# Two depthwise convolutions and the weight set-up of a two-layer state-space kernel: diagonal products for one convolution, set-up moved into the planned schedule

## The chip, the cores and the metric

The kernel runs on one core of a Trainium2 chip. Its time is the device time of one execution in microseconds; several executions are made and the median is given. Besides, one execution is recorded by the hardware profiler. The core has five engines with instruction queues of their own: TensorE (PE in the profile, its weight loads as PEld), VectorE (DVE), ScalarE (ACT), GpSimd (POOL) and SyncE (SP), which here only starts DMAs. A name with a q, such as SPq or ACTq, is an instruction that an engine's queue issues, a DMA above all.

## The reference, cut to what matters

The input is x of 4 images with 256 channels and 64 x 64 points, so 4 sequences of 4096 tokens. Layer 0 is a selective state-space block with a causal convolution of 4 taps in front of its recurrence. Layer 1 is a state-space block with 8 heads and scalar decays, again with such a convolution, and after it a feed-forward layer with 8 experts, each token going to one of them. The two convolutions are what the change touches:

```
# layer 0: xm has 512 channels
xp = jnp.pad(xm, ((0, 0), (K - 1, 0), (0, 0)))
xc = sum((xp[:, k:k + L, :] * conv_w[:, k] for k in range(K))) + conv_b
xm = jax.nn.silu(xc)
...
# layer 1: xBC has 512 channels of x and 128 of B and C
xpad = jnp.pad(xBC, ((0, 0), (D_CONV - 1, 0), (0, 0)))
conv = sum((xpad[:, k:k + L, :] * conv_w[:, k] for k in range(D_CONV))) + conv_b
xBC = jax.nn.silu(conv)
```

Everything is float32. A convolution here is depthwise: each channel has its own 4 weights.

## The kernel before, in words

**Phases.** Three phases follow one another: `mixers` (both state-space layers and the routing of the tokens), `experts` (71 blocks of 256 tokens through the feed-forward layer), and `turn` (the result is turned back to channels first and written out). The change lies in `mixers` alone.

**Chunks.** `mixers` works on 64 chunks of 256 tokens, 16 per sequence. For a chunk, `front0` (L712) makes the projections of layer 0 and its convolution, `mid0` (L764) the step sizes and inputs of the recurrence, `scan` (L824) the recurrence itself as 16 scans of 128 x 1024 on VectorE, `tail0` (L902) the output projection. `front1` (L924) makes the normalization, projections and convolution of layer 1, `ssd` (L1037) its state step in two halves of 128 tokens, and `back1` (L1127) its output, the choice of expert and the scatter of the rows into the routing buffer. Layer 1 works two chunks behind layer 0 (`lag = 2`, L1232).

**The order of the work.** `mixers` does not issue its instructions where they are written. `r` is a `Plan` (L136): each call of `r.mm`, `r.act`, `r.dve`, `r.gps` or `r.dma` notes an operation with a slot, and `k_.at(n)` sets the slot to 16 times the chunk's number plus n. `Plan.order` (L273) then goes through a simulated time: on each engine it starts the operation with the lowest slot that is ready and for whose tiles a buffer is free. The cost of an operation is charged by formulas in `mm`, `act`, `dve` and `gps` (L207 to L248). For `mm` with over 64 output rows this is `max(0.224, n / 592)` us, with up to 32 rows `max(0.15, n / 1500)`; for `dve` it is 0.06 us plus n / 960, and 0.14 instead of 0.06 where n is at most 4. The queues that come out are fixed: each engine takes its instructions in this order. All instructions of the plan are issued at one line, L371, so the profile tells them apart by tile names only.

**Buffers.** A tile has a ring with a name and a number of buffers. `raw`, the input of a convolution with 3 columns of the chunk before in front of it, is one buffer for both layers; `raw4` has three, `z` and `xn1` one each. In PSUM, layer 0 takes its banks from ring a (two), layer 1 from ring b (one), the state step from ring c (two).

**The convolution before.** Both layers do it alike. `to_taps` (L677) stores `raw` to DRAM as `raw_d`; `tapped` (L683) loads it back four times for each of 4 blocks of 128 channels, shifted by one column each time, so that the 128 partitions of `raw4` hold 4 taps of 32 channels; `convolve` (L693) makes 4 products with 128 rows of input and 32 columns of weights, each for 32 channels. The weights, `taps_m` for layer 0 and `taps_x` for layer 1, are made at the start by GpSimd from `sum4` (four 32 x 32 identities on top of one another) and the tap weights (L517). The much smaller convolution of B and C in layer 1 uses diagonal matrices, `diag_bc` (L510, L1019): 4 products of 128 x 128 that add up in PSUM, one for each tap, reading `rbc` at four shifts.

**The set-up before.** L442 to L596 stand ahead of the plan, so their instructions are the first in every queue. The weights of layer 0 are loaded from SP (L442 to L456), those of layer 1 from ScalarE's queue (L460 to L474). ScalarE has the Exp of `neg_a0` (L457) in front of these loads and the Exp of `neg_a1` (L475) behind them. Then come the products that fold the input projection and the means into the weights (L527 to L570), and those of layer 1 and of the gate (L573 to L592).

Of the kernel before, what the change touches and what calls it, by code (L numbers as in the profile page):

```python
# [20 lines left out]
P = 128  # L21
T = 256
# [82 lines left out]
class Root:  # L105


    def __init__(self, ring, depth, make, psum):
        self.ring, self.depth, self.make, self.psum = ring, depth, make, psum
        self.tile = self.first = None  # L110
        self.seen = []
        self.left = 0
        self.until = 0.0
        self.begun = ring is None

    def place(self):
        if self.tile is None:
# [18 lines left out]
class Plan:  # L136
# [30 lines left out]
    def note(self, engine, weight, f, args, kw, outs, ins, join=None, lag=0.0, port=False, ride=False):  # L167
        op = self.ops[-1] if join is not None and self.open == (join, self.now) else None
        if op is None:
            op = Op(len(self.ops), engine, self.now, self.step)  # L170
            self.ops.append(op)
        self.open = (join, self.now) if join is not None else None
        op.calls.append((f, args, kw))
        op.weight += weight
        op.lag = max(op.lag, lag)
        op.port, op.ride = op.port or port, op.ride or ride
        for parts, writes in ((ins, False), (outs, True)):
            for p in parts:
# [12 lines left out]
                root.seen.append((op, writes, p.box))  # L191
        return op


# [35 lines left out]
    def dve(self, name, *args, **kw):  # L230
        out, *rest = (*args, *kw.values())
        tensors = [a for a in rest if isinstance(a, Part) or hasattr(a, "ap")]
        n = max(self.width(a) for a in (out, *tensors))
        port = len([a for a in tensors if self.on_sbuf(a) and self.width(a) > 1]) > 1
        if name == "tensor_tensor_scan":
            n, port = 2 * n, False
        op = self.note("DVE", (0.06 if n > 4 else 0.14) + n / 960, getattr(self.nc.vector, name), args, kw, (out,), rest, port=port)
        op.scan = name == "tensor_tensor_scan"
        if op.scan:
            self.scans.append(op)  # L240
# [141 lines left out]
def tile_conv_attn_hybrid(ctx: ExitStack, tc: tile.TileContext, a: dict, out: bass.AP, cap: int, st: int):  # L382
# [12 lines left out]
    def nm(s):  # L395
        return f"{s}_{next(names)}"
# [27 lines left out]
    def mixers(es):  # L424
# [16 lines left out]

        w_in = load("w_in")  # L442
        w_gate = load("w_gate")
        b_gate = load("b_gate")
        ln_g = load("ln_g")
        ln_b = load("ln_b")
        m_in = load("m_in_w")
        m_cw = load("m_conv_w")
        m_cb = load("m_conv_b")
        m_xp = load("m_xproj_w")  # L450
        m_dtw = load("m_dt_w")
# [2 lines left out]
        m_d = load("m_D")  # L454
        m_out = load("m_out_w")
        w_out = load("w_out")  # L456
        act(neg_a0, neg_a0, AF.Exp)  # L457
        ts(neg_a0, neg_a0, -1.0, None, ALU.mult)

        s_in = wp.tile([P, KC, 2 * DI + 2 * N2 + NH + NE], F32, name="w_W_in", tag="w_W_in")  # L460
        nc.scalar.dma_start(s_in[:, :, :-NE], a["W_in"])
        s_cw = load("conv_w", nc.scalar)
        s_cb = load("conv_b", nc.scalar)
        s_cwbc = load("conv_w_bc", nc.scalar)
        s_cbbc = load("conv_b_bc", nc.scalar)
        s_dtb = load("dt_bias", nc.scalar)
        neg_a1 = load("A_log", nc.scalar)
        s_d = load("Dp", nc.scalar)
        s_gn = load("gnorm_w", nc.scalar)
        s_nw = load("norm_w", nc.scalar)  # L470
        s_out = wp.tile([P, KD, C + NE], F32, name="w_W_out", tag="w_W_out")
        nc.scalar.dma_start(s_out[:, :, :C], a["W_out"])
        g_w = load("gate_w", nc.scalar)
        g_b = load("gate_b", nc.scalar)  # L474
        act(neg_a1, neg_a1, AF.Exp)  # L475
        ts(neg_a1, neg_a1, -1.0, None, ALU.mult)

        for k in range(KC):
            ts(s_in[:, k, :-NE], s_in[:, k, :-NE], s_nw[:, k : k + 1], None, ALU.mult)
        for k in range(KD):  # L480
            ts(s_out[:, k, :C], s_out[:, k, :C], s_gn[:, k : k + 1], None, ALU.mult)
# [27 lines left out]
        diag_d1 = diagonal(s_d, "diag_d1")  # L509
        diag_bc = diagonal(s_cwbc, "diag_bc")  # L510
# [6 lines left out]
        def taps(scales, name):  # L517

            t = wp.tile([P, NG, R], F32, name=name, tag=name)
            for g in range(NG):  # L520
                nc.gpsimd.tensor_scalar(t[:, g], sum4, scales[:, g : g + 1], None, ALU.mult)
            return t
# [50 lines left out]
        g_cen = g_w  # L573
        pt_s = bank_a()
        for k in range(KC):
            mm(pt_s[:, :NE], mean_c, g_w[:, k], start=k == 0, stop=k == KC - 1)
        for k in range(KC):
            tt(g_cen[:, k], g_w[:, k], pt_s[:, :NE], ALU.subtract)

        nc.scalar.copy(s_in[:, :, -NE:], g_cen)
        for k in range(KD):
            pt_s = bank_a()
            for m in range(KC):
                nc.tensor.transpose(pt_s[:, m * P : (m + 1) * P], s_out[:, k, m * P : (m + 1) * P], ident)
            turned = wk.tile([P, KC, P], F32, name=nm("turned"), tag="sq", bufs=1)
            nc.scalar.copy(turned, pt_s[:, :C].rearrange("p (m l) -> p m l", m=KC))
            pt_s = bank_a()
            for m in range(KC):  # L590
                mm(pt_s[:, :NE], turned[:, m], g_cen[:, m], start=m == 0, stop=m == KC - 1)
            nc.scalar.copy(s_out[:, k, C:], pt_s[:, :NE])  # L592
# [38 lines left out]

        def scratch(shape, tag):
            return r.tile(lambda: dram2.tile(shape, F32, name=nm(tag), tag=tag), shape, tag, 3)

        routed, rows_at, ws_at = r.fixed(buf_d), r.fixed(row_at), r.fixed(w_at)

# [75 lines left out]
        def front0(k_):  # L712
# [28 lines left out]
            for half in range(2):  # L741
# [182 lines left out]
        def front1(k_):  # L924
# [510 lines left out]
def layouts(i):  # L1435
# [13 lines left out]

    def by_tap(w):  # L1450

        return np.asarray(w).reshape(NG, R, TAPS).transpose(2, 1, 0).reshape(P, NG)

    def spread(v):
# [24 lines left out]
        "conv_w": by_tap(at["conv_w"][:DI]),  # L1479
# [46 lines left out]
```

## Time and profile before

| | us |
|---|---|
| median of 3 executions | 6781.04 (6777.89 to 6788.52) |
| the profiled execution, its time | 6786.87 |
| its span, first to last instruction | 6785.2 |
| mean granted TensorE clock in it | 0.934 of full speed |

One instruction of TensorE on float32 appears as two passes in the profile, so the counts there are twice those of the code. A mean duration of a TensorE pass [...]overlaps with the pass after it; busy time is the union. A wait is put down to the engine and tile whose work came last before the waiting instruction started. The largest group of VectorE is the scans, 1024 of 2284 ns; the largest of GpSimd the product of the states with C (`p<-h,bc`), 1024 of 2357 ns; the largest of ScalarE the decays (`da<-dt,w_m_Alog`), 4096 of 502 ns. On the DMA side, the loads `raw<-raw_d` of both convolutions are 2048 transfers of 128 KB with a median of 3.8 us from issue to landing, and the stores `raw_d<-raw` are 128 of 518 KB with 4.2 us.

### The profile page before, as it was taken

The numbers are of one execution on the slowest core, as the hardware profiler recorded it, in microseconds if no ns is written. First come the engines' busy times: TensorE is split into PE (matmuls) and PEld (weight loads), VectorE is DVE, ScalarE is ACT, GpSimd is POOL, SyncE is SP. The second block draws the span as 40 slices with busy tenths as digits, with TensorE's granted clock in tenths as the row PEclk, the third lists the DMA queues.
The fourth block names the chain that finished last, engine by engine and source line by source line (L and its number), as shares of the span: only waits on it lengthen the run. The fifth ranks groups of instructions, "written<-read, shape, count | busy, mean of one in ns | idle before, by whom it ended". The sixth has DMA issues, their size and how long they took to land. (4 is left out here: it accounts for less than half of the span.)

```text
span 6785.2 us, 114276 instructions
## 1 busy us (share of the span) xinstructions
PE 5984.4 (88%) x37672; PEld 4045.8 (60%) x37672; DVE 5545.7 (82%) x7646; ACT 4859.2 (72%) x12007; POOL 3494.2 (51%) x2632
## 2 busy tenths in 40 slices
PE   5788888888888888888888888888888877999996
PEld 3455555555555555555555555555555546888885
DVE  3889999999999999999999999999999973344333
ACT  4778888888888888888888888888888852333332
POOL 3555555555555555555555555555555552333331
PEclk7889999999999999999999999999999988999998
DMA  6976777777777777777777777777777734555556
GB/s 177 254 184 179 183 181 181 181 184 184 181 181 177 180 181 183 184 182 182 183 182 183 183 183 181 184 183 183 183 183 181 178 102 152 193 193 191 187 194 243
DMA packets 1125138, 1245.58 MB, mean 184 GB/s; under 512 B 111888, under 2 KB 1093652, under 8 KB 1115330
## 3 DMA queue, kind: packets, MB, share of 16 engines
q1 hardware_dynamic: 1083458, 1008.76, 59.1%
q0 software_dynamic: 30000, 210.98, 8.8%
q10 hardware_dynamic: 11088, 18.53, 0.7%
q8 instruction: 300, 4.92, 0.3%
q14 instruction: 292, 2.39, 0.1%
HBM read 919.92 MB, written 311.63 MB: 182 GB/s over the span
## 5 line engine op out<-in xcount | busy, mean ns | idle before, releaser
L371 POOL TENSOR_TENSOR p<-h,bc 128x1024 f32<-128x1024 f32 x1024 | 2413.3, 2357 | 1995.3 <-DVE ub L371 578.3
L371 DVE TENSOR_TENSOR_SCAN h<-da,ub 128x1024 f32<-128x1024 f32 x1024 | 2338.9, 2284 | 80.4 <-ACT da L371 4.8
L371 ACT ACTIVATE da<-dt,w_m_Alog 128x255 f32<-128x255 f32 x4096 | 1830.7, 502 | 0.5 <-issue 0.5
L371 DVE TENSOR_TENSOR ub<-u,bc 128x1024 f32<-128x1024 f32 x1024 | 1269.1, 1239 | 20.2 <-DMA u<-u_d 11.3
L371 PE MATMUL py<-p,sum 128*32 128x256 f32 x8192 | 689.6, 411 | 334.1 <-POOL p L371 326.3
L371 PE MATMUL b<-t,w_W_in 128*128 128x256 f32 x2304 | 581.5, 393 | 65.1 <-ACT raw L371 26.1
L371 PEld LDWEIGHTS py<-p,sum 128*32 128x32 f32 x8192 | 180.7, 111 | 724.6 <-POOL p L371 465.2
L371 PEld LDWEIGHTS b<-t,w_W_in 128*128 128x128 f32 x2304 | 420.8, 191 | 230.6 <-ACT raw L371 90.3
L1374 PE MATMUL ph<-xt,w 128*128 128x256 f32 x2272 | 517.8, 381 | 5.2 <-ACT hid L1376 5.0
L1385 PE MATMUL po<-w,hid 128*128 128x256 f32 x2272 | 502.0, 379 | 0.0
L371 PE MATMUL a<-t,w_m_in_w 128*128 128x256 f32 x2048 | 496.6, 391 | 4.5 <-DVE t L371 4.5
L371 ACT COPY hlast<-h 128x4 f32<-128x4 f32 x1024 | 202.6, 198 | 407.3 <-DVE h L371 402.8
L1385 PEld LDWEIGHTS po<-w,hid 128*128 128x128 f32 x2272 | 431.7, 190 | 58.7
L1374 PEld LDWEIGHTS ph<-xt,w 128*128 128x128 f32 x2272 | 427.4, 191 | 64.8 <-ACT hid L1376 7.6
L371 PEld LDWEIGHTS a<-t,w_m_in_w 128*128 128x128 f32 x2048 | 377.0, 191 | 125.8 <-issue 50.6
L1351 DVE CAST number<-rows 128x2 uint32<-128x2 f32 x71 | 12.2, 172 | 486.0 <-DMA tok_d<-fixed,number 473.6
L371 PE MATMUL c<-cum,after 128*128 128x512 f32 x512 | 331.2, 752 | 83.8 <-ACT dend L371 67.3
L1349 ACT ACTIVATE tn<-rows 128x256 f32<-128x256 f32 x142 | 82.2, 597 | 421.0 <-DMA rows<-buf_d,row_at 420.6
L1397 POOL DMA_INDIRECT tok_d<-fixed,number x142 | 145.8, 1027 | 396.3 <-DVE fixed L1395 306.1
L371 ACT ACT_TABLE_LOAD x256 | 328.4, 1283 | 4.4
L371 ACT ACTIVATE cum<-upto,da 128x128 f32<-128x128 f32 x1024 | 328.7, 395 | 0.7 <-DVE da L371 0.7
L1376 ACT ACTIVATE hid<-ph,w 128x256 f32<-128x256 f32 x426 | 187.4, 468 | 143.7 <-PE ph L1374 143.1
(237 smaller groups left out, 11289.3 us busy)
## 6 DMA issues: line engine op xcount, KB each, us to landing
raw<-raw_d SPq DMA_DIRECT2D x2048, 128.0 KB, 3.8
dt<-dt_d SPq DMA_DIRECT2D x1024, 128.0 KB, 3.2
u<-u_d SPq DMA_DIRECT2D x1024, 128.0 KB, 3.9
raw_d<-raw SPq DMA_DIRECT2D x128, 518.0 KB, 4.2
gx_d<-pre SPq DMA_DIRECT2D x64, 1024.0 KB, 4.5
bc<-bc_d SPq DMA_DIRECT2D x1024, 64.0 KB, 2.4
gx<-gx_d SPq DMA_DIRECT2D x256, 256.0 KB, 5.2
dt_d<-mid SPq DMA_DIRECT2D x64, 512.0 KB, 2.9
```

The lines of the kernel that those rows point to most:

```text
L371: op.issued = f(*map(placed, args), **{k: placed(v) for k, v in kw.items()})
L1349: act(tn[:, j], rows[:, j, TOK:], AF.Identity, scale=rows[:, j, 1:2], bias=rows[:, j, 2:3])
L1351: nc.vector.tensor_copy(number, rows[:, :, 3])
L1374: mm(ph, w1[:, k, f * P : (f + 1) * P], xt[:, k], start=k == 0, stop=k == KC - 1)
L1376: act(hid[:, f], ph, AF.Relu, bias=b1[:, f : f + 1])
L1385: mm(po[:, j], hid[:, f, j * P : (j + 1) * P], w2[:, f], start=f == 0, stop=f == KF - 1)
L1397: nc.gpsimd.indirect_dma_start(out=tok_d, out_offset=bass.IndirectOffsetOnAxis(ap=number[:, j : j + 1], axis=0), in_=fixed[:, j], in_offse ...
```

## The change

Layer 0's convolution no longer goes through DRAM. `taps_m` becomes 16 diagonal matrices of 128 x 128 (one for each tap and each block of 128 channels), and `convolve` makes, for each block, 4 products that add up in one PSUM bank, reading `raw` in place at four shifts. Its store and its 16 loads per chunk are gone. Layer 1's convolution keeps the way through DRAM, under the name `convolve_taps`; its ring `raw4` has two buffers instead of three. `xn1` takes its buffer from the ring `z`.

The set-up of layer 1 (its loads, scalings, the gate's products, `taps_x`, `diag_bc`, `diag_d1`) is noted in the plan with slots from -22 to 0, its loads on SP. The Exp of `neg_a0` goes behind the set-up of layer 0, and the loads of layer 0 change their order: `m_in`, `ln_b`, `m_cw` and `ln_g` go ahead of `b_gate`. The tiles that the planned set-up makes are marked `lasting`: readers of them are no longer recorded, the writers stay. The charge of VectorE operations on up to 4 elements is 0.1 us instead of 0.14. In the tables of weights, `by_tap` now orders by block and tap, and `by_row` is the old `by_tap`.

```diff
-                root.seen.append((op, writes, p.box))
+                if not root.lasting:
+                    root.seen.append((op, writes, p.box))
...
-        op = self.note("DVE", (0.06 if n > 4 else 0.14) + n / 960, getattr(self.nc.vector, name), args, kw, (out,), rest, port=port)
+        op = self.note("DVE", (0.06 if n > 4 else 0.1) + n / 960, getattr(self.nc.vector, name), args, kw, (out,), rest, port=port)
...
         w_in = load("w_in")
         w_gate = load("w_gate")
+        m_in = load("m_in_w")
+        ln_b = load("ln_b")
+        m_cw = load("m_conv_w")
+        ln_g = load("ln_g")
         b_gate = load("b_gate")
...
-        act(neg_a0, neg_a0, AF.Exp)
-        ts(neg_a0, neg_a0, -1.0, None, ALU.mult)
-
-        s_in = wp.tile([P, KC, 2 * DI + 2 * N2 + NH + NE], F32, name="w_W_in", tag="w_W_in")
-        nc.scalar.dma_start(s_in[:, :, :-NE], a["W_in"])
-        s_cw = load("conv_w", nc.scalar)
...
-        taps_m = taps(m_cw, "taps_m")
-        taps_x = taps(s_cw, "taps_x")
+        taps_m = diagonal(m_cw, "taps_m")
...
-        mm(py, ident, s_in[:, 0, :512], start=True, stop=True)
+        mm(py, ident, m_in[:, 0, :512], start=True, stop=True)
...
+        def later(n, name, shape=None):
+            r.slot(n)
+            src = a[name]
+            t = r.fixed(wp.tile(list(shape or src.shape), F32, name=f"w_{name}", tag=f"w_{name}"))
+            r.dma("SP", t if shape is None else t[:, :, : src.shape[-1]], src)
+            return t
+
+        def later_diagonal(n, scales, name):
+            k = scales.shape[1]
+            t = r.fixed(wp.tile([P, k, P], F32, name=name, tag=name))
+            for i in range(k):
+                r.slot(n + 0.2 * i)
+                r.gps("tensor_scalar", t[:, i], ident, scales[:, i : i + 1], None, ALU.mult)
+            return t
+
+        s_in = later(-22, "W_in", [P, KC, 2 * DI + 2 * N2 + NH + NE])
+        s_nw = later(-22, "norm_w")
+        s_out = later(-18, "W_out", [P, KD, C + NE])
...
+        taps_x = r.fixed(wp.tile([P, NG, R], F32, name="taps_x", tag="taps_x"))
+        for g in range(NG):
+            r.slot(-6)
+            r.gps("tensor_scalar", taps_x[:, g], sum4, s_cw[:, g : g + 1], None, ALU.mult)
+        diag_bc = later_diagonal(-2, s_cwbc, "diag_bc")
+        diag_d1 = later_diagonal(0, s_d, "diag_d1")
+        r.slot(-8)
+        r.act(neg_a1, neg_a1, AF.Exp)
...
+        for t in (s_in, s_out, s_cb, s_cbbc, s_dtb, neg_a1, g_b, taps_x, diag_bc, diag_d1):
+            t.root.lasting = True
...
-            t = work([P, SQ, T], "raw4", 3)
+            t = work([P, SQ, T], "raw4", 2)
...
-        def convolve(raw4, weights, j, dst, bias, get):
+        def convolve_taps(raw4, weights, j, dst, bias, get):
             pi = get(T)
             for i in range(SQ):
                 r.mm(pi[i * R : (i + 1) * R], weights[:, j * SQ + i], raw4[:, i], start=True, stop=True)
+            r.act(dst, pi, AF.Identity, bias=bias[:, j : j + 1])
+
+        def convolve(raw, weights, j, dst, bias, get):
+            pi = get(T)
+            for k in range(TAPS):
+                r.mm(pi, weights[:, j * TAPS + k], raw[:, j, k : k + T], start=k == 0, stop=k == TAPS - 1)
             r.act(dst, pi, AF.Identity, bias=bias[:, j : j + 1])
...
                 if half == 0:
                     keep(raw, "raw0")
-                    d = to_taps(raw, "raw0_d")
             for j in range(KD):
                 k_.at(FRONT0 + 5 + j)
-                part = tapped(d, j)
                 k_.at(FRONT0 + 7 + j)
-                convolve(part, taps_m, j, pre0[:, KC + KD + j], m_cb, bank_a)
+                convolve(raw, taps_m, j, pre0[:, KC + KD + j], m_cb, bank_a)
...
-            xn1 = work([P, NS, C], "xn1")
+            xn1 = work([P, NS, C], "z")
...
-                convolve(part, taps_x, j, pre1[:, KD + j], s_cb, bank_b)
+                convolve_taps(part, taps_x, j, pre1[:, KD + j], s_cb, bank_b)
```

More of the change, by code (lines that the diff above doesn't have):

```diff
@@ L114, in __init__ @@
         self.begun = ring is None
+        self.lasting = False
     def place(self):
@@ L443, in mixers @@
         w_gate = load("w_gate")
+        m_in = load("m_in_w")
+        ln_b = load("ln_b")
+        m_cw = load("m_conv_w")
+        ln_g = load("ln_g")
         b_gate = load("b_gate")
[L445 to L448, printed above, removed]
         m_cb = load("m_conv_b")
@@ L456, in mixers @@
         w_out = load("w_out")
-        act(neg_a0, neg_a0, AF.Exp)
-        ts(neg_a0, neg_a0, -1.0, None, ALU.mult)
-        s_in = wp.tile([P, KC, 2 * DI + 2 * N2 + NH + NE], F32, name="w_W_in", tag="w_W_in")
-        nc.scalar.dma_start(s_in[:, :, :-NE], a["W_in"])
-        s_cw = load("conv_w", nc.scalar)
[L463 to L481, printed above, removed]
         def filled(value, shape, name):
@@ L507, in diagonal @@
             return t
-        diag_d1 = diagonal(s_d, "diag_d1")
-        diag_bc = diagonal(s_cwbc, "diag_bc")
         sum4 = wp.tile([P, R], F32, name="sum4", tag="sum4")
@@ L515, in mixers @@
             tt(sum4, sum4, ident[:, i * R : (i + 1) * R], ALU.add)
[L517 to L522, printed above, removed]
-        taps_m = taps(m_cw, "taps_m")
-        taps_x = taps(s_cw, "taps_x")
+        taps_m = diagonal(m_cw, "taps_m")
         pt_s = bank_a()
@@ L570, in mixers @@
             ts(m_in[:, k], m_in[:, k], ln_g[:, k : k + 1], None, ALU.mult)
[L573 to L592, printed above, removed]
+        act(neg_a0, neg_a0, AF.Exp)
+        ts(neg_a0, neg_a0, -1.0, None, ALU.mult)
         py = py_p.tile([P, 512], F32, name="py0", tag="py", bufs=1)
-        mm(py, ident, s_in[:, 0, :512], start=True, stop=True)
+        mm(py, ident, m_in[:, 0, :512], start=True, stop=True)
         rank = wp.tile([P, NE], F32, name="rank", tag="rank")
@@ new lines, in mixers @@
+        s_in = later(-22, "W_in", [P, KC, 2 * DI + 2 * N2 + NH + NE])
+        s_nw = later(-22, "norm_w")
+        s_out = later(-18, "W_out", [P, KD, C + NE])
+        s_gn = later(-18, "gnorm_w")
+        g_w = later(-18, "gate_w")
+        s_cw = later(-17, "conv_w")
+        s_cwbc = later(-17, "conv_w_bc")
+        s_d = later(-17, "Dp")
+        s_cb, s_cbbc, s_dtb, neg_a1, g_b = (
+            later(-16, n) for n in ("conv_b", "conv_b_bc", "dt_bias", "A_log", "gate_b")
+        )
+        taps_x = r.fixed(wp.tile([P, NG, R], F32, name="taps_x", tag="taps_x"))
@@ new lines, in mixers @@
+        for g in range(NG):
[5 more added lines that the diff above has]
+        r.act(neg_a1, neg_a1, AF.Exp)
+        r.dve("tensor_scalar", neg_a1, neg_a1, -1.0, None, ALU.mult)
+        for k in range(KC):
+            r.dve("tensor_scalar", s_in[:, k, :-NE], s_in[:, k, :-NE], s_nw[:, k : k + 1], None, ALU.mult)
@@ new lines, in mixers @@
+        for k in range(KD):
+            r.dve("tensor_scalar", s_out[:, k, :C], s_out[:, k, :C], s_gn[:, k : k + 1], None, ALU.mult)
+        pt_s = bank_c(NE)
+        for k in range(KC):
+            r.mm(pt_s, mean_c, g_w[:, k], start=k == 0, stop=k == KC - 1)
+        for k in range(KC):
+            r.tt(g_w[:, k], g_w[:, k], pt_s, ALU.subtract)
+        r.copy(s_in[:, :, -NE:], g_w)
+        for k in range(KD):
+            pt_s = bank_c(KC, P)
+            for m in range(KC):
+                r.transpose(pt_s[:, m], s_out[:, k, m * P : (m + 1) * P], ident)
+            turned = work([P, KC, P], "sq")
+            r.copy(turned, pt_s)
+            pt_s = bank_c(NE)
+            for m in range(KC):
+                r.mm(pt_s, turned[:, m], g_w[:, m], start=m == 0, stop=m == KC - 1)
+            r.copy(s_out[:, k, C:], pt_s)
@@ L1450, in by_tap, with by_row @@
     def by_tap(w):
+        return np.asarray(w).reshape(KD, P, TAPS).transpose(1, 0, 2).reshape(P, KD * TAPS)
+    def by_row(w):
         return np.asarray(w).reshape(NG, R, TAPS).transpose(2, 1, 0).reshape(P, NG)
@@ L1478, in layouts @@
         "W_in": blocks(at["W_in"].T),
-        "conv_w": by_tap(at["conv_w"][:DI]),
+        "conv_w": by_row(at["conv_w"][:DI]),
         "conv_b": cols(at["conv_b"][:DI]),
```

## The prediction

> **What bounds the kernel now.** I read the page first, then busy time by stage, then VectorE's waits in the long steady stretch, then the timeline of the first 112 us, then single shapes. The page:
>
> ```profile
> span 6785.2 us, 114276 instructions
> PE 5984.4 (88%) x37672; PEld 4045.8 (60%) x37672; DVE 5545.7 (82%) x7646; ACT 4859.2 (72%) x12007; POOL 3494.2 (51%) x2632
> ```
>
> No engine is full over the span, so I look by stage. Busy time in three windows (start:end, length, busy of PE, PEld, DVE, ACT, POOL with instruction counts, granted clock, DMA share, GB/s):
>
> ```profile
> 0.00:50.00 50.00, 25.72 (x94) 20.60 (x94) 7.93 (x26) 8.05 (x19) 20.60 (x63) 1.00 0.33 102
> 200.00:300.00 100.00, 78.32 (x492) 48.11 (x490) 83.77 (x89) 77.25 (x193) 49.90 (x34) 0.89 1.04 262
> 2000.00:3000.00 1000.00, 891.95 (x5940) 568.40 (x5938) 931.38 (x1246) 823.23 (x2063) 569.87 (x405) 0.94 0.72 181
> ```
>
> In the steady stretch VectorE is busy 93.1%, TensorE 89.2%. The first scan starts at 111.86 us and the last (the 1024th) at 5546.20 us, so a chunk of 16 scans takes (5546.2 - 111.9) / 1023 x 16 = 85.0 us: VectorE works 79.2 us of it and idles 5.8, TensorE 75.8 and 9.2. Three parts add up: 112 us to the first scan, 5434 us of scans, 1239 us for the last scans' successors, the experts and the output. What VectorE waits for between 1000 and 5300 us (us in total, times, longest), 50.6 chunks:
>
> ```profile
> DVE xdt L371 <- PE c L371: 71.6, 118, 2.6
> DVE state L371 <- PE c L371: 51.7, 44, 1.2
> DVE gm L371 <- PE c L371: 29.2, 39, 2.6
> DVE pre L371 <- PE c L371: 14.1, 40, 0.6
> ```
>
> These four are 166.6 us, 3.3 us a chunk, all on TensorE's products in the second layer's state step. No DMA is in that list at all. So in the steady stretch VectorE is the bound, TensorE a close second through these waits, and the DMA traffic hides.
>
> **The change, part by part.** *Set-up.* The timeline of the head (start, us, engine, line; in brackets the idle time before it):
>
> ```profile
> 10.49 0.65 ACTq L461 DMA_DIRECT2D w_W_in<-in_W_in_dram  x1
> ...
> 21.75 0.57 ACT L535 COPY w_nat<-bank_a 128x512 f32<-128x512 f32 x1
> 22.37 3.78 PE L540 MATMUL bank_a<-w_w_gate,w_nat 128*128 128x256 f32 x8 [17.62 <-ACT w_nat L535]
> 25.95 6.83 PE L567 MATMUL bank_a<-w_ln_b,w_m_in_w 128*128 128x1 f32 x32
> 43.58 2.64 PE L371 MATMUL a<-xin,w_cen 128*128 128x256 f32 x8
> ...
> 58.09 0.37 SPq L371 DMA_DIRECT2D raw_d<-raw  x1
> 61.90 7.46 SPq L371 DMA_DIRECT2D raw<-raw_d  x16
> 73.49 1.08 PE L371 MATMUL a<-raw,taps_m 128*32 128x256 f32 x8 [1.19 <-DMA raw<-raw_d]
> ```
>
> TensorE has finished its first transposes at 4.75 us and then waits for a copy on ScalarE that stands behind the Exp of m_Alog, which waits for its load until 10.49, and 13 weight loads issued on ScalarE's queue. All of these leave its front: the Exp is placed after, the 13 loads go to SP inside the plan, where SP is free from 10.5 to 48 us; 13 x 0.5 us of issue fit, behind the first chunk's xin. New chain: copy about 4.9-5.5, the w_gate product 3.78 -> 9.3, the 32 narrow products 6.83 -> 16.1 (m_in is now the third load; DMA moved 132 then 251 GB/s in the first two 5 us windows, 1.9 MB by 10 us, so it is there), copy 0.17 and VectorE's scaling 1.45 -> 17.9, the py0 product 2.05 -> about 20. The first chunk starts at 20 instead of 43.6: **-23.7 us**. If m_in lands late, 3 less. GpSimd's taps_m grows from 16 x 0.36 to 16 x 0.72 us (row diag_d, 2.89 for 4), 5 to 17 us, needed at about 37; taps_x, diag_bc and diag_d (12 us) follow it and end near 32, before the first tail_raw copy. The second layer's set-up work (TensorE: 18 small instructions, ScalarE 2.5 us, VectorE 3.5 us) now sits between the first chunk's steps; in the order of the built program most of it falls where TensorE waited for ScalarE or VectorE (idle 0.5 to 1.8 us at each step); I charge 1 us for the rest, and 5 as the upper end.
>
> *First chunk's convolution.* Now from 60.6 (m_in products done) to 75.15 through DRAM. After: 4 groups of 4 products, 32 passes at 8.86/32 = 0.277 us as m_in had at that point, 8.9 + 0.7 -> 9.6 instead of 14.6: **-5.0**. Then the store raw_d<-raw of chunk 1 no longer stands ahead of the fourth u load on SP (issued at 106.27 and 106.70); but ScalarE's decay tile is ready only at 111.3, so -1 (0 to -2). Head: -23.7 + 1 - 5 - 1 = **-29 us** (-20 to -33).
>
> *The crowded stretch.* From 140 to 400 us the DMA share is at 1.0 (clearing the routing buffer), and VectorE is busy 219.5 of 260 us against 242 at the steady rate: 23 us lost. The change takes 518 + 16 x 128 KB = 2.57 MB a chunk off, 30 of 260 GB/s. Bounds 0 and -23, nothing here gets later; I take half: **-12 us**.
>
> *TensorE in the steady state.* The convolution's shapes from 1000 to 5300 us (x counts passes, two an instruction), then two starts from the timeline:
>
> ```profile
> L371 PE MATMUL a<-raw,taps_m 128*32 128x256 f32 x1616 | 151.1, 452 | 0.0
> L371 PE MATMUL b<-rbc,diag_bc 128*128 128x256 f32 x408 | 101.8, 392 | 40.0 <-ACT pre L371 40.0
> ...
> 3046.60 1.89 PE L371 MATMUL b<-t,w_W_in 128*128 128x256 f32 x8
> 3048.42 0.64 PE L371 MATMUL py<-p,sum 128*32 128x256 f32 x8
> ```
>
> Before, 151.1 / 50.5 chunks = 3.0 us. After, four groups like diag_bc, 101.8/51 = 2.0 each: 8.0 us. So **+5.0 us of TensorE a chunk**. The Trainium skill speaks against this: "TensorEngine Tiling (Array Packing)", Theoretical Speedup, gives up to 4x to a stationary side of 32 columns, which is just what is given up. By that rule the old 3.0 would become 12.0, +9.0 a chunk, which would use up the whole 9.2 us of idle TensorE. The rows say 2.7x (and 1.82 against some 0.6 us between starts, 3x), the old groups being partly alone in the queue; I go by the rows. TensorE: 75.8 + 5.0 = 80.8 of 85.0, still under the period.
>
> Where it stands decides. In the built order all taps_m work falls into the state step, about 1.9 us of extra queue for each half of a chunk. It stands mainly between the two halves of the cum sums (472 of 1024 instructions), ahead of cc x bcs (248) and after the transposes of pre (224), the last under 2.5 us of VectorE work that must come first anyway. Ahead of gm that is 1.6 us more TensorE queue than before (2.9 against 1.35), so the gm wait (0.6 us a chunk) may double. Against that VectorE now has more of its own work between the scaled xdt and the state update that needs the product of it: 1.9 or 3.2 us by the half instead of 1.1 (scan 2.29, product 1.23 and so on), which covers most of the state wait of 1.0 us a chunk. The xdt wait (1.4) has 4.7 or 7.5 us of cover instead of 5.3: even. Sum -0.8 + 0.6 - 0.2 for a warmer clock.
>
> *The clock.* "TensorE: Matmul & The Clock Gate", The HAM clock gate, says an idle window of some 3.4 us halves the clock. The rows show such dips where TensorE waits: 0.80 at 3080-3085 (busy 2.4 of 5 us), 0.50 at 3165-3170, 0.94 on average, and 1.00 when the experts keep it full. By the rule a full queue would give all 6% of 76 us back, 4.6 us, nearly the whole +5.0; by the rows the dips sit where POOL's p and dend are late, which the change does not move; I take the 0.2 above. Steady state: **-0.4 us a chunk x 62 = -25 us**. Ends: -1.5 and +1.6 a chunk.
>
> *Edits at nothing.* 17 fewer DMAs a chunk on SP (97 to 80): hidden, as the waits show. raw stays in use until the last taps_m product, and the other layer's halo copy on GpSimd then waits for TensorE; behind it are p and so py. The slots leave 4 of 16 (21 us) on each side; cover gone, a late copy would hold p by 1-3 us a chunk. xn1 in z's ring waits for nothing that its input does not wait for. raw4 with two buffers: loads land in 3.8 us, the second layer's products stand 2.5-4.6 us apart; SP may stand 1-3 us twice a chunk with dt and u loads behind it, and has 85 - 80 x 0.47 = 47 us free. The drain, 5546 to 5638, has that chain bare: +2 us. The changed charge of 0.1 for VectorE operations of up to 4 elements moves only the order. The experts and the output stay.
>
> Sum: 6786.87 (the profiled execution's own time, span 6785.2) - 29 - 12 - 25 + 2 = 6723; the median 6781.04 stands 5.8 below that execution: 6717, rounded to **6715**.
>
> **Rivals.** *The denser TensorE helps more* (0.23): waits fall by 1.5 us a chunk, the clock stays warm: -93 instead of -25, 6650. For: 166.6 of the some 195 us in VectorE's list are waits on c. Against: POOL's p wait stays. *Head gain given back* (0.14): +0.5 us a chunk, +31: 6770. *Slower* (0.10): TensorE becomes the bound inside the state step. The plan charges 256/592 = 0.43 us for a product that takes 0.50, so 16 more make TensorE later than planned, and VectorE, in a fixed order, waits at gm and xdt. Price: of the 3.8 us a chunk added to the queue of the state step, 1.6 uncovered is +99, 6840. It decides from (29 + 12 - 2)/62 = 0.6 us a chunk on. *The moved set-up still blocks the first chunk* (inside the likeliest case): head -10, 6735.
>
> **From cases to numbers.** The likeliest case has 0.53, its own range 6680-6750. Range 6640-6790: leaves out the slower case and the lower part of the first rival, 0.18. Changes within 0.2% (13.6 us) can't be told from none. Faster: 0.53 + 0.23 + 0.06 of the third case = 0.82; same 0.08, the rest of the third; slower 0.10.
>
> **What would show it.** First w_cen product near 20 us and first scan near 83; starts of first and last scan 5434 - 37 apart; taps_m at 8.0 us a chunk; TensorE near 95% and its clock at or over 0.94; VectorE's state wait nearly gone, its gm wait up to double. Wrong, if waits on c rise over 3.9 us a chunk, if a DMA or GpSimd's halo copy enters VectorE's list, or if the first scan starts after 95 us.

## The result and the profile after

The changed kernel takes 6746.49 us (median of 6, 6738.36 to 6755.17); the kernel before, on the same chip, 6778.53 us (6770.1 to 6788.52). The ratio is 0.9949, with a 95% interval of 0.9939 to 0.9959: 0.5% faster, 32 us in medians, where about 66 were forecast. The profiled execution took 6746.82 us, 40 less than that of before (6786.87), which lay some 8 us above its own median. All terms below are taken between these two profiled executions, so they add up to 40.

The page of the changed kernel:

```profile
span 6745.1 us, 111880 instructions
PE 6239.9 (93%) x37672; PEld 4330.6 (64%) x37672; DVE 5559.2 (82%) x7646; ACT 4878.5 (72%) x12007; POOL 3305.5 (49%) x2632
```

TensorE went from 5984.4 to 6239.9 us busy over the same number of passes, in a span 40 us shorter. The same three windows of it (start:end, length, busy of PE, PEld, DVE, ACT, POOL with counts, granted clock, DMA share, GB/s):

```profile
0.00:50.00 50.00, 37.50 (x159) 29.38 (x159) 8.37 (x27) 18.97 (x35) 25.05 (x65) 0.87 0.39 121
200.00:300.00 100.00, 90.63 (x612) 59.04 (x610) 94.36 (x104) 85.66 (x207) 60.18 (x38) 1.00 0.94 253
2000.00:3000.00 1000.00, 937.67 (x5950) 614.18 (x5948) 929.42 (x1222) 828.16 (x2054) 529.93 (x400) 0.96 0.54 149
```

The head is denser (TensorE 37.5 of 50 us, not 25.7). In the second window VectorE rose from 83.8 to 94.4 of 100 us. In the third, the steady stretch, TensorE has 94%, a warmer clock (0.96) and less DMA beside it (0.54, not 0.72), but VectorE has what it had. The starts of the scans place the 40 us:

| part | before | after | forecast | measured |
|---|---|---|---|---|
| span's start to first scan | 111.9 | 82.4 | -29 | -29.4 |
| first scan to scan 192 (12 chunks) | 1025.4 | 1003.0 | -12 | -22.4 |
| scan 192 to the last, 1023 (52 chunks) | 4408.9 | 4420.8 | -25 (over all 62) | +11.9 |
| last scan to the end | 1239.0 | 1238.9 | +2 | -0.1 |

All of the gain lies ahead of scan 192: 29 us in the head and 22 in the first 12 chunks. The other 52 take 12 us more. From scan 192 to 992 a chunk takes 85.24 us rather than 85.06: VectorE works 79.99 (79.86) and idles 5.24 (5.19); here and in the table below its semaphore instructions, 0.3 to 0.6 us a chunk, are counted as work. What VectorE waits for between 1000 and 5300 us (us in total, times, longest):

```profile
DVE cdec L373 <- ACT cdec L373: 67.5, 45, 3.4
DVE stats L373 <- PE b L373: 58.0, 51, 3.9
DVE xdt L373 <- PE c L373: 30.4, 97, 0.9
DVE row L373 <- PE c L373: 25.7, 21, 1.3
DVE gm L373 <- PE c L373: 16.5, 52, 0.8
...
DVE state L373 <- PE c L373: 1.0, 3, 0.3
```

Set beside the list of before: the four waits on ring c, 166.6 us then, are 48 us now (the wait of `pre` is 0.2). But three waits are new or grown: `cdec`, which was not in the list, and these two, in the kernel before:

```profile
DVE stats L371 <- PE b L371: 6.8, 3, 3.3
DVE row L371 <- PE c L371: 1.2, 1, 1.2
```

`cdec` and `stats` hold 2.5 us a chunk, a little more than the 2.3 that the four gave up, and `row` another 0.5. No DMA and no copy of GpSimd is in this list.

### The profile page after: what moved, and what is told of

It reads as the page before. It is cut to its first block, busy times and chain, and to the rows that moved or that the text cites. A ratio compares the mean times of both kernels' runs of the same rounds, so it can differ in the third digit from the quotient of the medians.

```text
span 6745.1 us, 111880 instructions
## 1 busy us (share of the span) xinstructions
PE 6239.9 (93%) x37672; PEld 4330.6 (64%) x37672; DVE 5559.2 (82%) x7646; ACT 4878.5 (72%) x12007; POOL 3305.5 (49%) x2632
## 5 line engine op out<-in xcount | busy, mean ns | idle before, releaser
L373 PE MATMUL py<-p,sum 128*32 128x256 f32 x8192 | 658.9, 394 | 175.1 <-POOL p L373 168.8
L373 PE MATMUL a<-t,w_m_in_w 128*128 128x256 f32 x2048 | 513.4, 395 | 3.0 <-DVE t L373 2.7
L373 PE MATMUL a<-raw,taps_m 128*128 128x256 f32 x2048 | 482.0, 383 | 4.9 <-ACT pre L373 4.9
L373 PEld LDWEIGHTS a<-raw,taps_m 128*128 128x128 f32 x2048 | 378.2, 190 | 130.4 <-ACT e L373 39.8
L1362 ACT ACTIVATE tn<-rows 128x256 f32<-128x256 f32 x142 | 82.3, 597 | 402.9 <-DMA rows<-buf_d,row_at 397.2
L373 ACT ACT_TABLE_LOAD x256 | 328.4, 1283 | 4.5
```

The source lines that it names most:

```text
L373: op.issued = f(*map(placed, args), **{k: placed(v) for k, v in kw.items()})
L1362: act(tn[:, j], rows[:, j, TOK:], AF.Identity, scale=rows[:, j, 1:2], bias=rows[:, j, 2:3])
```

## Two shapes to read before the experiments

**The new wait at cdec.** A timeline of one such place in the changed kernel (start, us, engine, line, names; in brackets the idle time before):

```profile
3058.86 2.08 PE L373 MATMUL c<-cum,after 128*128 128x512 f32 x2
...
3060.86 1.98 PE L373 MATMUL a<-pre,w_m_xproj_w 128*64 128x256 f32 x8
...
3062.77 1.12 PE L373 MATMUL c<-cum,after 128*128 128x512 f32 x2
...
3063.83 1.08 PE L373 MATMUL c<-cum,ones 128*64 128x512 f32 x4
...
3065.59 0.69 DVE L373 TENSOR_TENSOR cdec<-cdec,cc 128x512 f32<-128x512 f32 x1 [1.79 <-ACT cdec L373]
```

Between the two `cum` products TensorE does layer 0's next projection (1.98 us), so `cum,ones` starts at 3063.83, ScalarE's `cdec` follows, and VectorE stands 1.79 us. The wait is put down to ScalarE, but in this place TensorE's fixed order is behind it. The forecast looked at `gm`, behind the same queue, and not at this.

**An operation that is held.** Another timeline of the same kernel:

```profile
3048.63 2.36 POOL L373 TENSOR_TENSOR p<-h,bc 128x1024 f32<-128x1024 f32 x1
...
3049.47 2.59 DVE L373 TENSOR_TENSOR decay<-decay,gm 128x1024 f32<-128x1024 f32 x1
```

VectorE's `decay` product takes 1.22 us when nothing is beside it. Here it starts while GpSimd's `p` runs and takes 2.59: `p` ends at 3050.99, and `decay` ends 1.07 us later. So it does its work after `p`, and the profile shows the time before as busy. All 50 `decay` products that start during a `p` between 1000 and 5300 us end 1.08 us after it, to within 0.01. From scan 192 to 992, 49 of 100 are held so (mean 2.65 us, the others 1.22); in the kernel before 45 of 100, less deeply (mean 2.11). The Trainium skill, "SBUF — State Buffer", section "SBUF: two separate sides", says that VectorE, where its operation has two inputs in SBUF, and GpSimd use a shared pair of ports as an exclusive lock, and that the one that comes second blocks until the other's instruction is over. These ends agree with that; the ports themselves no trace shows. `Plan.order` keeps such operations of the two engines apart in its simulated time, so each held one is a place where the chip has left the plan. VectorE's busy time therefore holds hidden waits, and I read busy and idle together from here on.

## The experiments

The first question was where the 32 us come from and why the steady state gave nothing. My theory: head and traffic give the gain, and the products of 128 columns, which TensorE is charged too little for, turn old waits into new ones. The rivals: the steady loss is the work of one of the side edits (the charge of small operations, the moved set-up), it is operations held by GpSimd, or it is TensorE that has become the bound.

All kernels were timed beside the kernel before on the same chip. In the table "first 12" and "rest" are the stretches between scans 0, 192 and 1023 of the profiled execution; the chunk, with VectorE's busy and idle time in it, is from scans 192 to 992. These are of one execution each; the executions of one kernel differ by 5 to 28 us as a whole.

| kernel | median us | ratio to before (95%) | first scan | first 12 | rest | chunk | busy + idle |
|---|---|---|---|---|---|---|---|
| before | 6778.53 | 1 | 111.9 | 1025.4 | 4408.9 | 85.06 | 79.86 + 5.19 |
| after | 6746.49 | 0.9949 (0.9939-0.9959) | 82.4 | 1003.0 | 4420.8 | 85.24 | 79.99 + 5.24 |
| e1, set-up only | 6757.65 | 0.9969 (0.9957-0.9981) | 86.4 | 1018.2 | 4415.8 | 85.18 | 79.93 + 5.25 |
| e2, products only | 6761.32 | 0.9969 (0.9957-0.9981) | 104.3 | 1002.5 | 4415.6 | 85.14 | 80.20 + 4.94 |
| e3, charge 0.14 | 6741.18 | 0.9936 (0.9923-0.9950) | 81.2 | 1009.9 | 4422.6 | 85.25 | 80.18 + 5.08 |
| e4, dead loads | 6767.07 | 0.9979 (0.9969-0.9988) | 80.8 | 1020.2 | 4428.1 | 85.52 | 80.36 + 5.16 |
| e5, n / 520 | 6694.46 | 0.9880 (0.9865-0.9895) | 76.4 | 1007.2 | 4361.5 | 84.19 | 81.26 + 2.93 |
| e6, patience 40 | 8015.41 | 1.1825 (1.1809-1.1841) | 82.3 | 1199.6 | 5495.2 | 105.93 | 80.00 + 25.92 |
| e7, products doubled | 6785.79 | 1.0011 (1.0005-1.0018) | 86.4 | 1006.5 | 4455.8 | 86.02 | 81.35 + 4.68 |
| e8, n / 520 and 0.14 | 6653.25 | 0.9811 (0.9798-0.9824) | 75.4 | 986.2 | 4354.2 | 83.90 | 80.45 + 3.45 |
| e9, before with n / 520 | 6728.95 | 0.9923 (0.9908-0.9937) | 103.4 | 1015.0 | 4353.9 | 83.90 | 80.66 + 3.24 |
| e10, n / 480 and 0.14 | 6930.20 | 1.0221 (1.0208-1.0234) | 77.0 | 1022.1 | 4583.2 | 88.40 | 85.16 + 3.24 |
| e11, n / 555 and 0.14 | 6777.21 | 0.9996 (0.9988-1.0004) | 78.1 | 1010.1 | 4444.9 | 85.74 | 80.50 + 5.24 |

### e1 and e2: the two parts alone

e1 is the changed kernel with layer 0's convolution put back through DRAM (three buffers of `raw4`, `xn1` with a ring of its own, the charge of 0.14). e2 is the kernel before with the other part alone:

```diff
-        taps_m = taps(m_cw, "taps_m")
+        taps_m = diagonal(m_cw, "taps_m")
...
-            t = work([P, SQ, T], "raw4", 3)
+            t = work([P, SQ, T], "raw4", 2)
...
-                    d = to_taps(raw, "raw0_d")
-                part = tapped(d, j)
-                convolve(part, taps_m, j, pre0[:, KC + KD + j], m_cb, bank_a)
+                convolve(raw, taps_m, j, pre0[:, KC + KD + j], m_cb, bank_a)
...
-            xn1 = work([P, NS, C], "xn1")
+            xn1 = work([P, NS, C], "z")
```

> The set-up part alone: layer 1's set-up in the plan and the new load order, but layer 0's convolution through DRAM as before, three raw4 buffers, xn1 in its own ring, the old charge of 0.14. If the parts simply add (my theory), only the head moves: first scan 24 us earlier than before (near 88 us), the first 64 scans still take about 342 us, the steady period stays at 85.06 us a chunk, time about 24 us below before (6755). Rival: the set-up's place in the plan also reshuffles the whole order, and the crowded first four chunks or the steady state move by over 10 us too.

> The diagonal products alone, with two raw4 buffers and xn1 in the ring of z, the set-up and the charge as before. My theory: first scan 6 us earlier, the first 64 scans 33 us shorter (309), and TensorE's extra 4.5 us a chunk bring the steady period to 85.2 or more, +10 to +20 over the scans: about 20 to 25 us below before (6757). Rival: the products themselves cost nothing or help in the steady state, and the loss there comes from the other edits: period 84.7 or less, about 60 us below before (6720).

Each part gives 0.3%, at a different place. The set-up moves the first scan by -25.5 us and the first 12 chunks by -7.2. The products move the first scan by -7.6 and the first 12 chunks by -22.9. In the rest both are 7 us over the kernel before, 0.1 us a chunk. VectorE's waits from 1000 to 5300 us tell the parts apart; first e1:

```profile
DVE xdt L373 <- PE c L373: 74.8, 120, 2.6
DVE state L373 <- PE c L373: 51.7, 44, 1.2
```

Then e2:

```profile
DVE cdec L371 <- ACT cdec L371: 74.1, 49, 3.3
DVE stats L371 <- PE b L371: 40.6, 49, 3.9
```

e1 waits as the kernel before does (71.6 and 51.7); e2 has the new waits. So the exchange of waits comes with the products and the two rings changed for them, and the moved set-up leaves the steady state alone. That e1 has the waits of before and still takes 0.1 us a chunk longer says how much of the +0.18 between the two kernels may be mere spread from run to run.

### e3: the charge of small VectorE operations

```diff
-(0.06 if n > 4 else 0.1) + n / 960
+(0.06 if n > 4 else 0.14) + n / 960
```

> The changed kernel with the old charge of 0.14 us for VectorE operations of up to 4 elements. My theory, that TensorE's load makes the new waits: within 10 us of the changed kernel (6746), the waits of stats on PE b and of cdec on ACT stay at 1 us a chunk or more. Rival, that the smaller charge spoilt the order: 20 us or more faster than the changed kernel, these waits gone.

Steady chunk 85.25 against 85.24, and the intervals overlap: alone, this edit does nothing that can be measured in the time. The waits are those of the changed kernel (`cdec` 72.9 us, `stats` 47.6). e3 is also e1 with the products and their rings, and nothing else: between these two the first scan moves by -5.2 us, the first 12 chunks by -8.3 and the rest by +6.8, 16 us in medians.

### e4: the traffic kept, without use

The changed kernel still stores `raw` and makes layer 0's 16 loads a chunk, but nothing reads them.

```diff
                     keep(raw, "raw0")
+                    d = to_taps(raw, "raw0_d")
             for j in range(KD):
                 k_.at(FRONT0 + 5 + j)
+                tapped(d, j)
                 k_.at(FRONT0 + 7 + j)
```

> The changed kernel with layer 0's store to DRAM and its 16 loads a chunk still made, though nothing reads what they bring: the DMA traffic of before beside the new products. My theory, that the first four chunks were freed by the DMA bytes taken off: the first 64 scans take 330 us or more again (309 in the changed kernel), the steady period moves by less than 0.2 us a chunk, time about 6775. Rival, that the freed order of the queues and not the traffic did it: first 64 scans within 8 us of 309, time within 10 us of 6746.

The first 12 chunks take 1020.2 us: of the 22.4 us won there, 17.2 are gone again. Three windows of the crowded stretch, 140 to 400 us (busy of PE, PEld, DVE, ACT, POOL; clock; DMA share; GB/s), first of the kernel before:

```profile
140.00:400.00 260.00, 199.73 (x1234) 123.74 (x1234) 219.46 (x239) 193.03 (x474) 130.05 (x89) 0.84 0.94 240
```

of the changed kernel:

```profile
140.00:400.00 260.00, 227.72 (x1449) 148.98 (x1451) 242.97 (x297) 214.65 (x541) 159.60 (x107) 0.96 0.77 213
```

and of e4:

```profile
140.00:400.00 260.00, 214.68 (x1298) 141.98 (x1299) 229.81 (x270) 195.46 (x492) 137.40 (x96) 0.91 0.89 233
```

VectorE's busy time goes 219, 243, 230 and the DMA share 0.94, 0.77, 0.89. VectorE had been short by 23 us against its steady rate, and the changed kernel has all of it back. So the traffic is part of what holds this stretch. The order is another part, because e3, without this traffic and with another order, stays in between too:

```profile
140.00:400.00 260.00, 229.42 (x1368) 149.72 (x1362) 232.87 (x284) 203.35 (x510) 142.48 (x99) 0.90 0.77 208
```

Its first 64 scans take 326.7 us, almost those of e4 (328.4), where the changed kernel takes 309.0 and the kernel before 341.7. Over 12 chunks the two groups do part: 1015.0 to 1025.4 us for the four kernels with the traffic (before, e1, e4, e9), 986.2 to 1010.1 for those without it (e6 and e10 aside, whose chunks are long throughout). The pairs that differ by it say 22.9 us (before, e2), 17.2 (e4, after) and 8.3 (e1, e3). In the rest the same loads cost 7.3 us, 0.14 a chunk over 52 chunks (0.28 from scan 192 to 992), little more than e1's spread: there they are nearly hidden.

### e5: TensorE charged 0.49 us

After e1 to e4 my theory was that the steady gain is lost because TensorE falls behind the plan, which charges 0.43 us for a product for which I had read 0.50. A charge of 256 / 520 = 0.49 should then take waits away. The 0.50 is too long: it holds the end of a group of four, which overlaps with the product after it. In the changed kernel:

```profile
3048.67 1.89 PE L373 MATMUL a<-raw,taps_m 128*128 128x256 f32 x8
3050.49 0.64 PE L373 MATMUL py<-p,sum 128*32 128x256 f32 x8
```

The next product starts 1.82 us after the first of the four, 0.46 a product; that is the median of 147 such groups from 1000 to 5300 us. It is 0.48 in e5, e8 and e11.

```diff
-        w = max(0.224, n / 592) if rows > 64 else ...
+        w = max(0.224, n / 520) if rows > 64 else ...
```

> The changed kernel, but the plan charges a TensorE product of 256 columns and over 64 rows at 0.49 us (n / 520) instead of 0.43, close to the 0.50 of the trace. If VectorE's waits in the steady state come from TensorE being later than planned (my theory): idle VectorE falls from 5.2 to 4.7 us a chunk or less, period 84.8 or less, some 25 us faster than the changed kernel (6720). Rival, that the waits only move as they did between before and after: period within 0.2 of 85.24, time within 15 us of 6746.

VectorE's idle time falls from 5.24 to 2.93 us a chunk, and only 7 of 101 `decay` products are held (mean 1.33 us). A part comes back: the 16 `ub` products a chunk go from 19.9 to 22.4 us. Net 1.05 us a chunk, and 52 us in medians, twice the 25 that I had expected.

### e6: GpSimd held back longer

The rival explanation was the held operations. The plan keeps `p` back until it can start with a scan, beside which it holds nothing, but at most `PATIENCE` us.

```diff
-    PATIENCE = 4.0
+    PATIENCE = 40.0
```

> The changed kernel with GpSimd's product p held for up to 40 us (4 before) until it can start beside a scan. My theory, that p running beside decay's product lengthens it and costs VectorE 0.6 us a chunk more than before: decay falls from 1.92 to under 1.4 us, VectorE's busy time by about 1 us a chunk, period to 84.5, time to about 6710. Rival, that the time is not set by this: decay gets short but p and so py come late, period 85.0 or more, time 6740 or more.

No `decay` is held any more (1.220 us), and the kernel is 18% slower: VectorE idles 25.9 us a chunk. The waits of GpSimd from 1000 to 5300 us begin with this:

```profile
POOL p L373 <- DVE mid L373: 805.0, 41, 21.0
```

`p` stands up to 21 us, `py` on TensorE waits 635 us for `p`, and the rest follows. The held operations are the price for `p` in time, and a much smaller one.

### e7: how much more TensorE can take

The first two blocks' products are made twice on halved weights, which gives the same sum: 8 more products a chunk.

```diff
+        for i in range(2 * TAPS):
+            nc.gpsimd.tensor_scalar(taps_m[:, i], taps_m[:, i], 0.5, None, ALU.mult)
...
-            for k in range(TAPS):
-                r.mm(pi, weights[:, j * TAPS + k], raw[:, j, k : k + T], start=k == 0, stop=k == TAPS - 1)
+            twice = 2 if j < 2 else 1
+            for n in range(twice * TAPS):
+                k = n % TAPS
+                r.mm(pi, weights[:, j * TAPS + k], raw[:, j, k : k + T], start=n == 0, stop=n == twice * TAPS - 1)
```

> The changed kernel with the products of the first two blocks of layer 0's convolution made twice on halved weights, the same sum: 8 products more a chunk, some 3.8 us of TensorE. My theory, that TensorE still has 5 us a chunk free and VectorE sets the period: period up by 0.6 us at most, time by 40 us at most (under 6790). Rival, that TensorE's queue already sets the period through the waits: period up by 3 us or more, time over 6930.

The group of products (x counts passes; busy us, mean ns) in e7, from 1000 to 5300 us:

```profile
L373 PE MATMUL a<-raw,taps_m 128*128 128x256 f32 x2396 | 563.1, 384 | 0.0
```

563.1 / 50 = 11.3 us a chunk against 7.5 in the changed kernel. For these 3.8 us of TensorE a chunk is 0.79 us longer, a little over the 0.6 expected. But VectorE idles less (4.68, not 5.24); what grew is its busy time, by 1.36: `ub` +1.7 for being held more often, `decay` -0.8. So even with 3.8 us more, and TensorE busy 94.8% of the steady window at a clock of 0.98, TensorE is not what ends last. The order that came out holds VectorE more.

### e8 and e9: the two kernels with one charge

e8 is the changed kernel with the edits of e5 and e3 together, e9 the kernel before with n / 520 (its small operations are at 0.14 anyway). These two differ by the change alone, without its 0.1.

> The changed kernel with the charge of 0.49 us for a product of 256 columns and the old 0.14 us for small VectorE operations. If each charge nearer to the trace helps: faster than either alone, under 6720. If the order only moves waits about: between 6730 and 6760.

> The kernel before with the charge of 0.49 us (n / 520) for a product of 256 columns and over 64 rows; its 0.14 for small VectorE operations stays. If the plan's low charge hurts the more, the more such products there are (my theory): some 20 to 50 us below the kernel before (6735 to 6760), clearly less than the 87 us that both charges bring the changed kernel (6741 to 6653). Rival, that the charge helps any order alike: 80 us or more, 6700 or less.

Both have a chunk of 83.90 us, and 4354 us for the rest. Under this charge the products cost and give nothing in the steady state, although TensorE is busy 946.8 us of the 1000 in e8 and 901.0 in e9. The change is worth -28.0 us to the first scan, -28.8 in the first 12 chunks, +0.3 in the rest and +3 at the end, -53.5 between the profiled executions; in medians it is -76 (e9's executions lie between 6709 and 6737, and its profiled one near the low end). e8 is the fastest version of all, 1.9% under the kernel before. It differs from e5 by the charge of small operations alone, and is 41 us faster (6653 and 6694): the edit that did nothing in e3 is worth more than the whole change here. VectorE's waits in e8, 1000 to 5300 us:

```profile
DVE t L373 <- PE b L373: 63.4, 51, 2.3
DVE ex L373 <- PE c L373: 17.6, 24, 0.7
DVE state L373 <- PE c L373: 14.4, 44, 0.6
...
DVE cdec L373 <- ACT cdec L373: 0.2, 1, 0.2
```

The `cdec` wait, 67.5 us in the changed kernel, is 0.2: it belongs to one order and not to the products as such.

### e10 and e11: the charge to both sides

If a charge near the measured duration is what helps, 256 / 555 = 0.46, which is the distance between starts, should do well, and 256 / 480 = 0.53 do little harm. Each edit is that of e8 with 555 or 480.

> The changed kernel with 0.14 for small VectorE operations and the product charged above the trace's 0.50, at 0.53 us (n / 480). If the gain comes from a plan in which TensorE isn't later than thought, it stays: 6640 to 6690. If 6653 was one lucky order among many, this one lies anywhere from 6700 to 6760.

> The changed kernel with 0.14 for small VectorE operations and the product charged at 0.46 us (n / 555), between 0.43 (6741) and 0.49 (6653). By the theory of the charge between the two, 6680 to 6720; by luck of the order, anywhere from 6640 to 6760.

The theory falls: by charge, 0.43 gives 6741 us (e3), 0.46 gives 6777, 0.49 gives 6653, 0.53 gives 6930. The two charges nearest to the measured 0.46 to 0.48 stand 124 us apart. Half of it survives: VectorE's idle time is 5.1 and 5.2 at the two low charges and 3.5 and 3.2 at the two high ones. But the time in which VectorE is held varies as well. In e10 its busy time is 85.2 us a chunk, 4.7 above e8, by shapes such as these:

```profile
L373 DVE SCALAR_TENSOR_TENSOR mid<-mid,mid 128x1024 f32<-128x1024 f32 x49 | 128.2, 2616 | 0.0
...
L373 DVE TENSOR_TENSOR ratio<-ratio,scale 128x2 f32<-128x2 f32 x49 | 98.5, 2011 | 0.0
```

These take 1191 and 152 ns in the changed kernel. With a shift of 4 elements that went from 155 to 1833 ns they are 5 us a chunk. 43 of the 49 `ratio` products start during a `p` and end 0.02 us after it. Why one charge gives an order in which they meet `p`, and another one in which they do not, stays open.

## Why the prediction was half right

**Head (-29 forecast, -29.4 measured): right in sum, with terms that cancel.** The changed kernel's head, from its timeline:

```profile
4.84 0.59 ACT L501 COPY w_nat<-bank_a 128x512 f32<-128x512 f32 x1 [2.76 <-PE bank_a L498]
5.48 3.78 PE L506 MATMUL bank_a<-w_w_gate,w_nat 128*128 128x256 f32 x8 [0.68 <-ACT w_nat L501]
9.05 3.83 PE L533 MATMUL bank_a<-w_ln_b,w_m_in_w 128*128 128x1 f32 x32
14.78 0.43 DVE L527 TENSOR_SCALAR w_w_out<-w_w_out 128x512 f32<-128x512 f32 x1 [9.17 <-DMA w_w_out<-in_w_out_dram]
15.14 1.54 DVE L536 TENSOR_SCALAR w_m_in_w<-w_m_in_w,w_ln_g 128x1024 f32<-128x1024 f32 x2
17.91 2.78 PE L373 MATMUL a<-xin,w_cen 128*128 128x256 f32 x8
35.04 7.08 PE L373 MATMUL a<-raw,taps_m 128*128 128x256 f32 x32
```

The copy on ScalarE comes at 4.84, as forecast, and the chain behind it runs without a gap on TensorE up to the narrow products. The first chunk starts at 17.91 rather than 43.58, -25.7 for -23.7: the 32 narrow products took 3.83 us and not the 6.83 of before. Some 2 us of that were lost again, because VectorE's scaling of `m_in` stood behind that of `w_out`, which waited for its load until 14.78. The first convolution, from the end of `m_in` to the last `pre`, went from 14.55 to 7.4 us, -7.1 for -5.0. From there to the first scan it took 3.1 us more, where the forecast had +1 for the set-up steps in between and -1 for a load. The loss lies ahead of VectorE's first `mid` product, 18.3 us after the last `pre` and not 15.1; the projection to the step sizes (`a<-dbl,w_m_dt_w`) alone took 3.78 us at a granted clock of 0.50, where it had taken 1.99 at 1.00. The load did come earlier, but it gained nothing, because the first scan then stands 3.91 us for ScalarE's decays.

**Crowded stretch (-12 forecast, -22.4 measured): right mechanism, mis-sized.** The bounds were 0 and -23 and the half was taken; the far bound came true. Taking about a ninth of the traffic off (2.57 MB a chunk, 30 of 260 GB/s) let the whole shortfall go here, and e4 puts 17 of the 22 us down to the traffic. But in another order the same step is worth 8 us (e1, e3), so how much of the 22 is the order's stays open. In the kernel before the share of the stretch was 0.94, and not the 1.0 of the forecast, which its middle part has.

**Steady state (-0.4 a chunk forecast, +0.2 measured): the step that failed.** The forecast had -0.8 at `state`, +0.6 at `gm`, nothing at `xdt`. Measured a chunk, over 50.6 chunks: `state` (51.7 to 1.0) -1.0, `xdt` (71.6 to 30.4) -0.8, `pre` (14.1 to 0.2) and `gm` (29.2 to 16.5) -0.3 each, so these four did better than forecast. `mid` gave 0.5 more, in its wait and in being held less. All of it was given back at four places that the sum did not have: `cdec` +1.3, `stats` (6.8 to 58.0) +1.0, `row` (1.2 to 25.7) +0.5, and +0.6 in `decay` products that are held longer, the two shapes from 1000 to 5300 us being, in the changed kernel:

```profile
L373 PE MATMUL a<-raw,taps_m 128*128 128x256 f32 x1600 | 375.7, 382 | 0.0
...
L373 DVE TENSOR_TENSOR decay<-decay,gm 128x1024 f32<-128x1024 f32 x101 | 193.0, 1911 | 0.0
```

`decay` was 1623 ns before:

```profile
L371 DVE TENSOR_TENSOR decay<-decay,gm 128x1024 f32<-128x1024 f32 x100 | 162.3, 1623 | 0.3
```

The first line of the two above also says that the added TensorE work, 375.7 / 50 = 7.5 us a chunk for 3.0, was sized right (8.0 forecast, 95% busy against 93.8%). The sum went wrong because it followed the new work into the waits that were in the list of before, and a new fixed order makes waits where there were none. That the forecast 25 us did not come is clear; whether the small loss in their place is one, or spread, is not, because e1 without the products is 0.1 us a chunk up as well. And that the total still lay in the forecast range owes something to luck: the crowded stretch gave 10 us more than forecast, against the 37 that the steady state fell short.

**The rivals.** "Head gain given back" (+0.5 a chunk) is the nearest in kind: +0.18 was given back in the steady state, while the crowded stretch hid it in the total. "Slower, TensorE becomes the bound" needed 0.6 us a chunk; e9 beside e8 shows no cost in the steady state at 94.7% busy, and e7 shows no longer idle time of VectorE at 3.8 us more. Its ground, a product of 0.50 us against a charge of 0.43, was too large: by starts it is 0.46. "The denser TensorE helps more" had the clock right (0.96, not 0.94) and no gain from it. "The set-up still blocks" is excluded by the first product at 17.91.

## What to carry to other kernels

When an order is planned ahead from charges, cost a change by the stretch in which a resource is really full (here the head, and the chunks beside a nearly full DMA side), and give the steady state an uncertainty of its own: a charge changed by 7 to 8% moved this kernel by up to 4%, more than the change itself. Compare such a change under more than one charge before crediting it with a steady-state gain or loss. And read an engine's busy time by shape against the shortest time of that shape, since part of it can be waiting.

## What the runs showed of the hardware

A VectorE product of 128 x 2 elements took 2.01 us instead of 0.15 where it met GpSimd's `p` (2.36 us), and one of 128 x 1024 took 2.6 instead of 1.22: the price hangs on what is left of the GpSimd operation and not on VectorE's own size, since the one ends 0.02 us after `p` and a `decay` product 1.08. TensorE's granted clock from 2000 to 3000 us was mostly higher where TensorE was busier: 0.94 at 89.2% busy (before) and 0.92 at 90.1% (e9), 0.96 to 0.98 at 92.6% to 94.8% (e2, after, e8, e7). A chunk was no shorter for it: e3 and the changed kernel have 0.98 and 0.96, and 85.25 and 85.24 us. And 32 products with one column of output took 3.83 us in one place and 6.83 in the other, with the same operands and a granted clock of 0.98 and 1.00; why was not tried.
